# Expert rows: gathered inside the expert loop instead of scattered into per-expert lists ahead of it

## The chip, the cores and the metric

The kernel runs on one core of a Trainium2 chip. A core has engines that work side by side: TensorE for matmuls (PE in the profile, its weight loads PEld), VectorE (DVE), ScalarE (ACT) and GpSimd (POOL), and SyncE (SP), which here only issues DMAs. Each engine takes its instructions in order; engines wait for each other through semaphores. Data moves between HBM and the core's memories by DMA, issued by SP, ACT or POOL. The metric is the device time of one execution in microseconds, the median of several runs.

## The reference, cut to what matters

The input is 8 sequences of 256 tokens, 2048 tokens in all, of 128 features, in float32. One layer is a sandwich: half a feed-forward step, attention, half a feed-forward step with the same weights, and then a second, different layer (the tail). Each feed-forward step is a mixture of eight experts, of which every token uses two:

```python
h = rmsnorm(x @ W_in.T, in_norm_w)
logits = h @ Wr.T
_, idx = jax.lax.top_k(logits + expert_bias, TOP_K)
sel = jnp.take_along_axis(logits, idx, axis=-1)
```

For every token and each of its two experts, the row h is multiplied by the expert's gate and up matrices (128 to 512), goes through silu(gate) times up, and is multiplied by the expert's down matrix (512 to 128) and normed. The two results are weighed by the softmax of sel, normed, multiplied by W_out, and half of that is added to x. So 4096 pairs of token and expert are computed, and which tokens belong to which expert is known only at run time.

## The kernel before

**Order of work.** The program is a straight line: dispatch of the first feed-forward step, its expert loop, its combination, attention (with the second dispatch placed in its later steps), the second expert loop, its combination together with the tail. On PE, DVE, ACT and SP the instructions keep the order in which the program emits them. POOL's order is held for the instructions that ask for it.

**Dispatch** (L311 to L446), once for each group of 128-token tiles. The groups of the first step are `EARLY`, of the second `LATE`. `turned` transposes x, `product` multiplies by W_in and the router at once, `normed` and `scaled` (L373) write the normed row h twice into `hrow`, with the token's number in a 129th column, `choice` finds the two experts, and `places` (L399) counts with small products of 0/1 matrices which place the token has in each expert's list. From it comes `posi` (L428), the row in a DRAM array `hs` with one region of 2304 rows for each expert. `rows` (L430) scatters: for each tile and choice POOL issues one indirect DMA (L433) that writes 128 rows of 516 bytes to the places in `posi`. There are 32 of these in each step.

**Table** (L448 to L519). From the counts of the experts DVE works out which expert and which stretch of its list each of 24 fixed turns treats: 15 pairs of two blocks of 128 rows, and 9 singles. `tab` holds the expert and the first row of every turn, `far` is used to send lanes without a token out of bounds. In the first step, `zeros` (L521) writes zeros behind each expert's list; for the second step, `clear_rows` (L534) clears all of `hs` in 12 large DMAs on ACT's queue during attention.

**Expert loop** (L553 to L660). `fetch_weights` (L561) brings one expert's 832 KB, `fetch_rows` (L570) the turn's rows, both as plain DMAs on SP (L568, L574) with addresses read from `tab`. `turn_rows` transposes the rows (`pht`, L580), `gate` and `up` are `pg` and `pu` (L590), `down` is `py` (L613). Then ACT takes a sum of squares (`ysq`, L623), DVE writes `yrow` (L624), two DVE operations (L628, L631) work out the target row from the fetched token's number, and POOL scatters the result rows into `y2` (L633), one indirect DMA for each block, 39 in a loop. Weights and rows have four buffers, `yrow` two. One turn is:

```python
            sg = gate(t)
            if i + 1 < NT:
                turn_rows(TURNS[i + 1])
            up(t, sg)
            if i < len(pieces):
                pieces[i]()
            if i > 0:
                down(TURNS[i - 1])
            if i + 3 < NT:
                fetch_rows(TURNS[i + 3])
                fetch_weights(TURNS[i + 3])
```

`TURNS` repeats pair, pair, single seven times and ends with a pair and two singles. `pieces` are bits of other work put into the first loop, among them constants for attention that POOL fills with memsets (L800 to L822).

**Attention** is a list of steps, each with a part "a" and a part "b", in which pieces of the second dispatch are placed by hand (L997 to L1109); what remains of it follows after the last step.

Of the kernel before, what the change touches and what calls it, by code (L numbers as in the profile page):

```python
# [10 lines left out]
F32 = mybir.dt.float32  # L11
AF = mybir.ActivationFunctionType
ALU = mybir.AluOpType
# [27 lines left out]
REGION = NTOK + TT  # L41
HS_ROWS = E * REGION + 1
FAR = 1 << 20

EARLY = (0, 2), (2, 2), (4, 4), (8, 4), (12, 4)
# [10 lines left out]
TABLE = 2 * E + E * E + NSING * E + 2 * NT * E + NT + 3 * E  # L56
# [3 lines left out]
def macaron_kernel(ctx: ExitStack, tc: tile.TileContext, a: dict, out: bass.AP):  # L60
# [44 lines left out]
    def pack(name, widths, rows=P):  # L105
# [10 lines left out]
    win, wr_t, inw, eb, tri, slot, base, order, tokid = pack(  # L116
        "pack1", [D, E, 1, E, P, 2, E, E, NCH * TPC * 2]
    )
    tokid = tokid.rearrange("p (t k) -> p t k", k=2).bitcast(I32)
# [4 lines left out]
    zero = const.tile([P, 2 * ROW], F32, tag="zero", name="zero")  # L124
    nc.vector.memset(zero, 0.0)
# [7 lines left out]
    hss = [tc.dram_tile([HS_ROWS, ROW], F32, name=f"hs{f}") for f in range(2)]  # L133
# [170 lines left out]
    thr, upto, nth, tof, eof, tid, vals = cuts((2, E), (E, E), (NSING, E), (NT, E), (NT, E), (NT,), (3, E))  # L304

    hrows = [const.tile([P, TPC, 2, ROW], F32, tag=f"hrow{c}", name=f"hrow{c}") for c in range(NCH)]
    lsel = const.tile([P, NCH * TPC, 2], F32, tag="lsel", name="lsel")
    macc = const.tile([P, len(EARLY) + 1, E], F32, tag="macc", name="macc")
    nc.vector.memset(macc[:, 0, :], 0.0)

    def dispatch(f, i, parts, mp):  # L311
# [4 lines left out]
        x = xs[t0 // TPC][:, t0 % TPC : t0 % TPC + nt, :]  # L316
        hrow = hrows[t0 // TPC][:, t0 % TPC : t0 % TPC + nt]
        slots = slice(t0, t0 + nt)

        def turned():  # L320
            pt = bank(f"pxt_{n}", "sa")
            for t in range(nt):
                nc.tensor.transpose(pt[:, ts(t, P)], x[:, t, :], ident)
            st["xt"] = xntp.tile([P, CT], F32, tag="xnt", name=f"xnt_{n}")
            nc.scalar.copy(st["xt"][:, 0 : nt * P], pt[:, 0 : nt * P])
            st["u"] = mp.tile([P, TPC, D + E], F32, tag="u", name=f"u_{n}")[:, 0:nt]
            st["ss"] = small.tile([P, nt], F32, tag="ss", name=f"ss_{n}")

        def measured():
            bs = small.tile([P, nt, 6], F32, tag="ast", name=f"ast_{n}")  # L330
            mv = small.tile([P, nt, 2], F32, tag="amv", name=f"amv_{n}")
            for t in range(nt):
                nc.vector.bn_stats(bs[:, t, :], x[:, t, :])
# [5 lines left out]
        def product(i):  # L339
            if 2 * i >= nt:  # L340
                return
            pp = bank(f"pin_{n}_{i}", "sa" if f else None)[:, 0 : 2 * (D + E)]
            pp = pp.rearrange("p (j d) -> p j d", j=2)
            for j in range(2):
                nc.tensor.matmul(
                    pp[:, j, :], st["xt"][:, ts(2 * i + j, P)], win_r, start=True, stop=True
                )
            u = st["u"][:, 2 * i : 2 * i + 2]
            nc.scalar.copy(u, pp)
            sq = norm.tile([P, 2, D], F32, tag="sq", name=f"sqin_{n}_{i}")  # L350
            for j in range(2):
                t = 2 * i + j
                nc.scalar.activation(
                    sq[:, j], u[:, j, 0:D], AF.Square, accum_out=st["ss"][:, t : t + 1]
                )

        def normed():
            ri = small.tile([P, nt], F32, tag="ri", name=f"ri_{n}")
            nc.vector.scalar_tensor_tensor(ri, st["ss"], 1.0 / D, st["z"], ALU.mult, ALU.add)
            if f == 0:  # L360
                nc.vector.tensor_copy(hrow[:, :, :, D].bitcast(I32), tokid[:, slots])
# [5 lines left out]
            st["ri"] = ri  # L367

# [4 lines left out]
        def scaled(ts_=range(nt)):  # L373
            for t in ts_:
                u = st["u"][:, t, 0:D].unsqueeze(1).to_broadcast([P, 2, D])
                nc.scalar.activation(hrow[:, t, :, 0:D], u, AF.Copy, scale=st["ri"][:, t : t + 1])
# [22 lines left out]
        def places():  # L399
# [25 lines left out]
            pos = small.tile([P, nt, 2], F32, tag="pos", name=f"pos_{n}")  # L425
            nc.vector.tensor_reduce(pos, both, AX.X, ALU.add)
            st["posi"] = small.tile([P, nt, 2], I32, tag="posi", name=f"posi_{n}")
            nc.vector.tensor_copy(st["posi"], pos)  # L428

        def rows(ts_=range(nt)):  # L430
            for t in ts_:
                for k in range(2):
                    ins = nc.gpsimd.indirect_dma_start(  # L433
                        out=hss[f],
                        out_offset=bass.IndirectOffsetOnAxis(ap=st["posi"][:, t, k : k + 1], axis=0),
                        in_=hrow[:, t, k, :],
                        in_offset=None,
                    )
                    tc.declare_no_dep(ins.ins, group=f"hs{f}", reason="rows of their own")
                    tc.add_to_no_dep_group(f"hs{f}", ins.ins)  # L440
                    tc.keep_in_program_order(ins)

        halves, choices = ([partial(p, i) for i in range(2)] for p in (product, choice))
        if f == 0:
            return turned, *halves, measured, both(normed, logits, scaled), *choices, places, rows
        return turned, *halves, measured, normed, logits, scaled, *choices, places, rows  # L446

    def table(f, parts, mp):  # L448
# [5 lines left out]
        pc = bank(f"pcnt_{f}", "sb")[:, 0:E]  # L454
# [3 lines left out]
        if f == 0:  # L458
            first = t_([P, E], "first", I32)
            nc.vector.tensor_tensor(first, pc, base, ALU.add)  # L460
            zeros(first)
# [1067 lines left out]
```

## Time and profile before

| | us |
|---|---|
| median of 3 runs (lowest, highest) | 659.83 (657.87, 660.45) |
| profiled execution | 673.83 |
| its span | 672.0 |
| dispatch and table of the first step, first loop's start | 0 to 76 |
| first expert loop | 76 to 190 |
| its combination | 190 to 210 |
| attention, most of the second dispatch in it | 210 to 420 |
| end of the second dispatch, table | 420 to 454 |
| second expert loop | 454 to 562 |
| combination and tail | 562 to 672 |

The profile is of one execution, which was some 14 us longer than the median of the others. All times below that name a place ("518.35") are microseconds from the start of its span. A line of the timeline gives start, length, engine, line of the source, operation and operands; in brackets stands how long the engine had been idle, and what ended the wait. `<-remote` and `<-issue` mean that the profile shows no work of this core that the engine waited for. A line of a group gives the number of instructions, their busy time and the mean in nanoseconds, and then the idle time before them. The shown length of a DMA is that of its issue.

### The profile page before, as it was taken

Reading aid. Unit: us, or ns where it says so; the run is one execution under the profiler, and the core shown is the slowest. Engines: PE = TensorE matmul, PEld = TensorE weight load, DVE = VectorE, ACT = ScalarE, POOL = GpSimd, SP = SyncE. Lnnn points to the kernel's source line nnn. Section 1 sums busy time; section 2 is a strip of 40 time slices with the busy share of each in tenths; the row PEclk is TensorE's granted clock in tenths of the full one; section 3 lists DMA queues with packets and bytes.
Section 4 is the critical chain, followed back from the end, with each engine's and each line's share of the span. In section 5 each row is a group of like instructions: output and inputs, shape, how many; then the busy total and the mean of one; then the engine's idle time right before and its main releaser. Section 6 shows DMA issues by size and latency. Waiting matters only on the chain.

```text
span 672.0 us, 11456 instructions
## 1 busy us (share of the span) xinstructions
PE 526.8 (78%) x3945; PEld 415.8 (62%) x3945; DVE 361.6 (54%) x1121; ACT 277.6 (41%) x682; POOL 196.0 (29%) x204
## 2 busy tenths in 40 slices
PE   4521499999957998898898758449999992679996
PEld 3521399999954545555555434329989992458885
DVE  3663156544433555766866545654444451667676
ACT  3451032323323454656664435313222331768355
POOL 0466056633332110101104052522233333511110
PEclk9999999999985799999999779559999997669999
DMA  5012746767721293984930000156767773100002
GB/s 208 32 43 99 248 139 195 240 208 230 230 83 45 41 168 61 148 130 72 143 64 25 9 32 13 36 171 203 239 191 231 237 233 94 50 0 1 1 1 62
DMA packets 57513, 78.26 MB, mean 116 GB/s; under 512 B 5035, under 2 KB 47570, under 8 KB 57328
## 3 DMA queue, kind: packets, MB, share of 16 engines
q1 hardware_dynamic: 33712, 59.02, 30.0%
q10 hardware_dynamic: 19200, 10.04, 9.7%
q0 software_dynamic: 4544, 8.47, 3.6%
q8 instruction: 31, 0.51, 0.3%
q14 instruction: 26, 0.21, 0.1%
HBM read 55.60 MB, written 22.83 MB: 117 GB/s over the span
## 4 chain that ended last, share of the span: by engine, by line
PE 60%; DVE 11%; ACT 9%; DMA 9%; issue 4%; another core or an unknown queue 3%; SPq 1%; POOL 1%; ACTq 0%; DVEq 0%; POOLq 0%
PE pg_f L590 10%; PE py_f L613 10%; PE pu_f L590 9%; PE ps L934 7%; PE po L981 3%; ACT es L971 3%; DMA qk<-heads 3%; PE pvf L1291 2%; PE pgo L1318 2%; DMA y<-yrow_f,idx_f 2%; PE pm L917 2%; DMA w_f<-in_wall_dram 2%; PE pk_m L1235 1%; PE pht_f L580 1%
## 5 line engine op out<-in xcount | busy, mean ns | idle before, releaser
L633 POOL DMA_INDIRECT y<-yrow_f,idx_f x78 | 76.4, 979 | 136.5 <-ACT sg_f L599 79.5
L433 POOL DMA_INDIRECT hs<-hrow,posi_f x64 | 61.9, 966 | 111.3 <-issue 38.2
L934 PE MATMUL ps<-qa,qk 32*128 32x256 f32 x512 | 75.4, 410 | 20.2 <-ACT es L971 17.3
L971 ACT ACTIVATE es<-ps 128x1024 f32<-128x1024 f32 x64 | 65.3, 1020 | 59.4 <-PE ps L934 35.3
L954 DVE TENSOR_REDUCE m<-pm 128x4 f32<-128x1024 f32 x64 | 77.7, 1220 | 20.5 <-PE pm L917 20.5
L917 PE MATMUL pm<-qk 32*128 32x256 f32 x512 | 79.7, 422 | 3.1 <-DMA qk<-heads 1.8
L590 PE MATMUL pg_f<-ht_f,w_f 128*128 128x256 f32 (+1 forms) x384 | 79.7, 352 | 2.9 <-DMA w_f<-in_wall_dram 2.2
L613 PE MATMUL py_f<-w_f,hg_f 128*128 128x128 f32 x624 | 78.2, 276 | 2.4 <-DVE yrow_f L624 2.4
L613 PEld LDWEIGHTS py_f<-w_f,hg_f 128*128 128x128 f32 x624 | 75.2, 192 | 4.6 <-DVE yrow_f L624 3.2
L590 PE MATMUL pu_f<-ht_f,w_f 128*128 128x256 f32 (+1 forms) x384 | 76.9, 344 | 0.0
L606 DVE TENSOR_TENSOR hg_f<-pu_f,sg_f 128x1024 f32<-128x1024 f32 (+1 forms) x48 | 49.2, 1024 | 47.0 <-PE pu_f L590 34.9
L590 PEld LDWEIGHTS pg_f<-ht_f,w_f 128*128 128x128 f32 x384 | 63.1, 197 | 9.6 <-issue 2.9
L934 PEld LDWEIGHTS ps<-qa,qk 32*128 32x128 f32 x512 | 44.5, 189 | 38.4 <-ACT es L971 29.4
L599 ACT ACTIVATE sg_f<-pg_f 128x1024 f32<-128x1024 f32 (+1 forms) x48 | 41.4, 863 | 62.2 <-PE pg_f L590 62.2
L623 ACT ACTIVATE ysq_f<-py_f 128x128 f32<-128x128 f32 x78 | 21.0, 274 | 110.7 <-PE py_f L613 93.4
L590 PEld LDWEIGHTS pu_f<-ht_f,w_f 128*128 128x128 f32 x384 | 61.8, 194 | 6.2
L917 PEld LDWEIGHTS pm<-qk 32*128 32x128 f32 x512 | 47.7, 195 | 7.3 <-issue 3.3
L624 DVE TENSOR_TENSOR yrow_f<-py_f,w_f 128x256 f32<-128x256 f32 (+1 forms) x48 | 18.0, 375 | 54.3 <-ACT ysq_f L623 54.2
L580 PE MATMUL pht_f<-ident,hst_f 128*128 128x128 f32 x78 | 17.5, 290 | 33.0 <-DMA hst_f<-hs 32.9
L582 DVE TENSOR_SCALAR ht_f<-pht_f,pack 128x256 f32<-128x256 f32 (+1 forms) x48 | 20.7, 431 | 33.4 <-PE pht_f L580 33.3
L981 PE MATMUL po<-es,v 128*32 128x256 f32 x512 | 36.6, 401 | 0.0
L966 DVE TENSOR_TENSOR qa<-pmt,qk 128x256 f32<-128x256 f32 x32 | 13.5, 422 | 38.4 <-PE pmt L960 28.9
(257 smaller groups left out, 832.5 us busy)
## 6 DMA issues: line engine op xcount, KB each, us to landing
w_f<-in_wall_dram SPq DMA_DIRECT2D x47, 832.0 KB
hs<-zero ACTq DMA_DIRECT2D x12, 774.0 KB
hst_f<-hs SPq DMA_DIRECT2D x30, 129.0 KB
y_f<-y SPq DMA_DIRECT2D x14, 258.0 KB
pack<-in_pack_dram SPq DMA_DIRECT2D x1, 1729.0 KB
heads<-qkc SPq DMA_DIRECT2D x3, 512.0 KB
qk<-heads SPq DMA_DIRECT2D x12, 128.0 KB
y<-yrow_f,idx_f POOLq DMA_INDIRECT x78
```

Source lines behind the costliest of these rows:

```text
L433: ins = nc.gpsimd.indirect_dma_start(out=hss[f], out_offset=bass.IndirectOffsetOnAxis(ap=st["posi"][:, t, k : k + 1], axis=0), in_=hrow[:, ...
L580: nc.tensor.transpose(pt[:, ts(s, P)], hst[t][:, s, 0:D], ident)
L590: nc.tensor.matmul(ph[:, k, :], w[t][:, o + k * P : o + k * P + P], ht[t], start=True, stop=True)
L599: nc.scalar.activation(sg, pg, AF.Silu)
L606: nc.vector.tensor_mul(hg[t], pu, sg)
L613: nc.tensor.matmul(py[:, s, :], hg[t][:, k, ts(s, P)], w[t][:, 2 * DFF + k * D : 2 * DFF + k * D + D], start=(k == 0), stop=(k == NFC - 1),)
L633: ins = nc.gpsimd.indirect_dma_start(out=y2, out_offset=bass.IndirectOffsetOnAxis(ap=idx[:, s : s + 1], axis=0), in_=yrow[:, s, :], in_off ...
L917: nc.tensor.matmul(sc[:, jj, i, :], qs[c][r, g, col + i * P : col + (i + 1) * P], ks[c][r, g, col : col + S], start=True, stop=True,)
L934: nc.tensor.matmul(sc[:, jj, i, :], ks[c][r, g, col + i * P : col + (i + 1) * P], tops[s][r, :], start=True, stop=True,)
L954: nc.vector.tensor_reduce(m, sc, AX.X, ALU.max, negate=True)
L971: nc.scalar.activation(es, sc, AF.Exp, scale=scale)
L981: nc.tensor.matmul(po[32 * j : 32 * j + 32, :], vs[c][:, (b % 2) * 2 + i, (g % 2) * (H // 2) + (g // 2) * 4 + j, :], ess[s, j // 2][:, j % ...
```

## The change

The lists are not made in DRAM any more. `hs` becomes a plain array of 2048 rows in the order of the tokens, 512 bytes each, written by a linear DMA on SP (`rows`). What is made instead is a list of token numbers in a tile of the core: for every block of the loop, lane by lane, the token that stands there.

The place of a token in its expert's list is cut into a block number (times 128) and a lane (0 to 127). `spread` makes two matrices for each tile and choice, by comparison with a row of counts: `hi` has the token's number plus one where the block number matches, `lo` has a one where the lane matches. The product of both, summed over tiles and choices by PE in PSUM (`mapped`), is a matrix that has in row "block" and column "lane" the token's number plus one, or zero. `maps` keeps one such matrix for each group of tiles. After the table, products of `maps` with 0/1 columns `sel` pick the rows of the blocks that the turns treat (`who`), and two bitwise operations make of it `lists`: the rows to gather from, and the rows to scatter to, out of bounds where there is no token.

In the loop `fetch_rows` is now one indirect DMA on POOL for each block, which gathers 128 rows from `hs` by `lists`; the scatter to `y2` takes its rows from `lists` too. Both keep POOL's program order. The zeros, the clearing and the index operations of the loop are gone. The table is shorter and its expert numbers are ready earlier. The groups of the first dispatch are 4, 4 and 8 tiles in place of 2, 2, 4, 4 and 4. The constants of attention are filled by POOL at the very start, not in the first loop, and the first weights are split into three DMAs in both loops.

```diff
-EARLY = (0, 2), (2, 2), (4, 4), (8, 4), (12, 4)
+EARLY = (0, 4), (4, 4), (8, 8)
...
-    hss = [tc.dram_tile([HS_ROWS, ROW], F32, name=f"hs{f}") for f in range(2)]
+    hss = [tc.dram_tile([NTOK, D], F32, name=f"hs{f}") for f in range(2)]
...
         def scaled(ts_=range(nt)):
             for t in ts_:
-                u = st["u"][:, t, 0:D].unsqueeze(1).to_broadcast([P, 2, D])
-                nc.scalar.activation(hrow[:, t, :, 0:D], u, AF.Copy, scale=st["ri"][:, t : t + 1])
+                nc.scalar.activation(
+                    st["hrow"][:, t], st["u"][:, t, 0:D], AF.Copy, scale=st["ri"][:, t : t + 1]
+                )
+
+        def rows():
+            dst = hss[f][t0 * P : (t0 + nt) * P, :].rearrange("(t p) c -> p t c", p=P)
+            nc.sync.dma_start(dst, st["hrow"])
...
-        def rows(ts_=range(nt)):
-            for t in ts_:
+            part = small.tile([P, 2, nt, 2], I32, tag="part", name=f"part_{n}")
...
+            nc.vector.tensor_copy(st["pos"], part)
+
+        def spread(engine=nc.gpsimd):
+            st["lo"], st["hi"] = (
+                mp.tile([P, nt, 2, P], F32, tag=k, name=f"{k}_{n}", bufs=1) for k in ("lo", "hi")
+            )
+            pos = st["pos"]
+            for t in range(nt):
                 for k in range(2):
-                    ins = nc.gpsimd.indirect_dma_start(
-                        out=hss[f],
-                        out_offset=bass.IndirectOffsetOnAxis(ap=st["posi"][:, t, k : k + 1], axis=0),
-                        in_=hrow[:, t, k, :],
-                        in_offset=None,
+                    tc.keep_in_program_order(
+                        nc.gpsimd.tensor_scalar(
+                            st["hi"][:, t, k],
+                            count128,
+                            pos[:, 0, t, k : k + 1],
+                            tokid[:, t0 + t, k : k + 1],
+                            ALU.is_equal,
+                            ALU.mult,
+                        )
                     )
+                    if engine is nc.gpsimd:
+                        tc.keep_in_program_order(
+                            nc.gpsimd.tensor_scalar(
+                                st["lo"][:, t, k], count, pos[:, 1, t, k : k + 1], None, ALU.is_equal
+                            )
+                        )
+            if engine is nc.vector:
+                row = count.unsqueeze(1).to_broadcast([P, 2, P])
+                for t in range(nt):
+                    nc.vector.tensor_tensor(
+                        st["lo"][:, t], bc_last(pos[:, 1, t], P), row, ALU.is_equal
+                    )
+
+        def mapped():
+            pm = bank(f"pmap_{n}", "sa" if f else None)[:, 0:P]
+            for t in range(nt):
+                for k in range(2):
+                    nc.tensor.matmul(
+                        pm,
+                        st["hi"][:, t, k],
+                        st["lo"][:, t, k],
+                        start=(t == k == 0),
+                        stop=(t == nt - 1 and k == 1),
+                    )
+            nc.scalar.copy(maps[:, i], pm)
...
-        far = t_([P, 2, NT, 2], "far", I32)
-        nc.vector.tensor_scalar(far[:, 0], free, -float(FAR - 1), float(FAR - 1), ALU.mult, ALU.add)
-        nc.vector.tensor_scalar(far[:, 1], free, float(FAR), None, ALU.mult)
-        return tab, far
-
-    def zeros(first):
...
-    def clear_rows(i, n):
...
+        who = bank(f"pwho_{f}", "sb")[:, 0:NBLK]
+        for i in range(len(parts)):
+            nc.tensor.matmul(who, maps[:, i], sel, start=(i == 0), stop=(i == len(parts) - 1))
+
+        num_ = t_([P, NBLK], "number", I32)
+        nc.vector.tensor_scalar(num_, who, -1.0, None, ALU.add)
+        lists = t_([P, 2, NBLK], "lists", I32)
+        sh = [P, 2, NBLK]
+        nc.vector.tensor_tensor(
+            lists, num_.unsqueeze(1).to_broadcast(sh), bc_last(bits[:, 0:2], NBLK), ALU.bitwise_and
+        )
+        return tab, lists
...
         def fetch_rows(t):
             n, m = f"f{f}_{t}", blocks(t)
-            row = nc.values_load(tab[0:1, 0, t : t + 1], engines=[SP], min_val=1, max_val=HS_ROWS - TT)
-            hst[t] = mp.tile([P, 2, ROW], F32, tag="hst", name=f"hst_{n}", bufs=4)[:, 0:m]
-            nc.sync.dma_start(hst[t], hss[f][bass.ds(row, m * P), :].rearrange("(s p) c -> p s c", p=P))
+            hst[t] = mp.tile([P, 2, D], F32, tag="hst", name=f"hst_{n}", bufs=4)[:, 0:m]
+            for s in range(m):
+                b = block(t, s)
+                tc.keep_in_program_order(
+                    nc.gpsimd.indirect_dma_start(
+                        out=hst[t][:, s, :],
+                        out_offset=None,
+                        in_=hss[f],
+                        in_offset=bass.IndirectOffsetOnAxis(ap=lists[:, 0, b : b + 1], axis=0),
+                    )
+                )
...
-            idx = mp.tile([P, 2], I32, tag="idx", name=f"idx_{n}", bufs=3)[:, 0:m]
-            nc.vector.tensor_tensor(
-                idx, hst[t][:, :, D].bitcast(I32), far[:, 0, t, 0:m], ALU.bitwise_and
-            )
-            nc.vector.tensor_tensor(idx, idx, far[:, 1, t, 0:m], ALU.bitwise_or)
...
-                    out_offset=bass.IndirectOffsetOnAxis(ap=idx[:, s : s + 1], axis=0),
+                    out_offset=bass.IndirectOffsetOnAxis(ap=lists[:, 1, b : b + 1], axis=0),
...
+                tc.keep_in_program_order(ins)
...
         for t in TURNS[:3]:
-            for fetch in (fetch_rows, fetch_weights) if f else (fetch_weights, fetch_rows):
-                fetch(t)
+            fetch_rows(t)
+            fetch_weights(t)
...
-                at(25, "a", places)
-                for i in range(TPC):
-                    at(25 + i, "b", partial(rows, [i]))
+                at(20, "b", rows)
+                at(25, "a", places, spread)
+                at(30, "a", mapped)
...
-            stagger([dispatch(0, i, EARLY, gp) for i in range(len(EARLY))], 4)
...
+                for piece in constant_pieces():
+                    piece()
+                with tc.tile_pool(name="front", bufs=2, reuse_waits="tile") as fp:
+                    stagger([dispatch(0, i, EARLY, fp, maps) for i in range(len(EARLY))], 4)
+                    decays[0]()
```

## The prediction

> **What bounds the kernel now.** I read the table of busy time and the chain that ended last first, then a table by stage, then the timeline of the places that the change touches. The page:
>
> ```profile
> span 672.0 us, 11456 instructions
> PE 526.8 (78%) x3945; PEld 415.8 (62%) x3945; DVE 361.6 (54%) x1121; ACT 277.6 (41%) x682; POOL 196.0 (29%) x204
> PE 60%; DVE 11%; ACT 9%; DMA 9%; issue 4%; another core or an unknown queue 3%; SPq 1%; POOL 1%; ACTq 0%; DVEq 0%; POOLq 0%
> L633 POOL DMA_INDIRECT y<-yrow_f,idx_f x78 | 76.4, 979 | 136.5 <-ACT sg_f L599 79.5
> L433 POOL DMA_INDIRECT hs<-hrow,posi_f x64 | 61.9, 966 | 111.3 <-issue 38.2
> ```
>
> PE carries 60% of the chain and POOL 1%, so POOL looks free. An average hides the stages (start:end and length, then PE, PEld, DVE, ACT, POOL busy, PE clock, DMA share, GB/s):
>
> ```profile
> 0.00:76.00 76.00, 23.89 (x97) 20.58 (x97) 36.61 (x205) 24.48 (x74) 31.64 (x41) 1.00 0.32 108
> 76.00:190.00 114.00, 113.14 (x750) 103.60 (x749) 55.19 (x149) 33.96 (x105) 50.66 (x51) 1.00 0.66 206
> 210.00:420.00 210.00, 177.63 (x1860) 108.17 (x1860) 126.81 (x288) 110.64 (x211) 33.69 (x33) 0.92 0.44 73
> 454.00:562.00 108.00, 104.16 (x715) 96.62 (x714) 46.53 (x117) 32.28 (x101) 37.18 (x38) 1.00 0.67 208
> ```
>
> The front (0 to 76) is a chain through DVE and POOL with PE idle; both expert loops (rows two and four) are full of PE work. What a loop can lose is idle PE. The order within one cycle, at turn ends (start, length, engine, line):
>
> ```profile
> 517.25 0.15 DVE L628 TENSOR_TENSOR idx_f<-hst_f,tab_far 128x2 int32<-128x2 int32 x1
> 518.35 0.98 POOL L633 DMA_INDIRECT y<-yrow_f,idx_f  x1 [4.77 <-ACT sg_f L599]
> 519.63 0.98 POOL L633 DMA_INDIRECT y<-yrow_f,idx_f  x1 [0.30 <-issue]
> 521.57 0.38 PE L580 MATMUL pht_f<-ident,hst_f 128*128 128x128 f32 x2
> 522.14 0.98 POOL L633 DMA_INDIRECT y<-yrow_f,idx_f  x1 [1.53 <-issue]
> 523.42 0.98 POOL L633 DMA_INDIRECT y<-yrow_f,idx_f  x1 [0.30 <-issue]
> ```
>
> The down projection of a pair ended at E = 516.05; its two scatters start at 518.35 and 519.63 (0.98 each, 0.30 between: a period of 1.28). The transposes at 521.57, E+5.5, use the rows that were fetched right after that down projection, today by SP, which POOL does not touch. And in the front:
>
> ```profile
> 42.31 0.96 POOL L433 DMA_INDIRECT hs<-hrow,posi_f  x1 [0.30 <-issue]
> 43.41 0.19 DVE L423 TENSOR_TENSOR at_row_f<-prank_f,pack 128x32 f32<-128x32 f32 x1 [4.70 <-remote]
> 62.83 0.38 DVE L499 TENSOR_REDUCE tab_single<-tab_room 128x27 f32<-128x216 f32 x1 [2.45 <-remote]
> ```
>
> DVE stands still 4.70 us until the eighth scatter in a row is done, and the table has eight such gaps while 16 more run: it takes 52.9 to 69.4 here, and 435.8 to 443.6 in the second dispatch, where few scatters run.
>
> **What the skill says.** "Perfetto Trace Analysis", DMA Instruction — SWDGE (GPSIMD): the shown interval of a DMA issued by POOL ends when its descriptors are made, not when data has moved. The trace agrees: 0.98 shown, 2.29 from start to landing for the last scatters of a loop (558.98, 563.07). "DMA: Bandwidth & Descriptors", Anatomy of one DMA — SWDGE (gpsimd) path: about 2.0 us fixed plus bytes/436e3, which for 64 KB of rows is an estimated 2.15; no gather from POOL is in the trace. "TensorE: Matmul & The Clock Gate", What's actually happening: an idle window of about 3.4 us halves PE's rate; here the first eight gate matmuls of a loop take 3.75 us against 1.73 warm.
>
> **The change part by part.** Sums are against the profiled run (673.8, span 672.0), which is 14 us above the median of 659.8; I carry the difference over to the median.
>
> *Both loops, the main step.* Removed: two index operations on DVE per turn (0.15 + 0.16 us, hidden by PE, but 0.26 of the lead to the scatter), the row fetches on SP. Added: 39 gathers per loop on POOL, in program order, the gather of turn i+3 queued behind the scatters of turn i-1, which wait for that turn's yrow. In the repeating cycle pair A, pair B, single C a turn's PE work is 4.57, 5.35 and 3.78 (gate and up 1.73 or 0.89 each, down 1.78 or 0.89, transposes 0.22 or 0.11), together the measured 13.70. After A's down ends at E: scatters at E+2.04 and E+3.32, gathers for the next B at E+4.60 and E+5.88. Needed: E + 3.78 + 1.73 = E+5.51. So even the start of the last gather is 0.37 late, and the stall is 0.37 plus its landing L. B's scatters, then C's one gather: starts at E+9.72, needed at E+10.08 plus the stall: fits. C's scatter and A's two gathers: 0.66 late at L = 2.3, which takes that much from the next stall at B. So one cycle loses 0.37+L in sum, and there are seven (the first three turns are fetched ahead). POOL has 78 × 1.28 = 100 us of work per loop of 107, so it cannot catch up by much.
> L is unknown. Low end: 1.5, if a read of 512-byte rows returns sooner than a scatter's 2.29 completion. High end: 5 to 5.9, which scatters took at three loaded moments (492.84 landed at 498.72). I take 3.0, nearer the unloaded value because weights fill two thirds of DMA time. 7 × 3.37 = 23.6 per loop; at 1.5 it is 13.1, at 5.0 it is 37.6. In loop 0 the placed pieces lengthen the window (its PE runs 114 against 107); I take 4 off. Two loops: **+43**.
>
> *Front.* Removed: 32 scatters, 8 zero fills on two queues, SP's wait for them (its first weight issue 69.83, rows 71.06 behind it, landed 75.4, first gate 76.73). Merging the last eight tiles and no DVE stall should bring the last posi from 52.9 to some 45.6 (4.7 for the stall, the rest ten-odd DVE operations of 0.2). Added behind it: 16 POOL operations of 128x128. None is in the trace: affine select 128x128 took 0.29, so I take 0.35 (5.6 us), bounds 0.15 and 0.6 (-3, +4); POOL ends at 51.5. The lo maps run on DVE meanwhile (8 × 0.42). Products keep up with POOL: +0.5, copy +0.4; the count for the table waits behind them on PE. Table to the expert numbers as in the second dispatch, 5.9: 58.3. Five operations and three products to the lists: 2: 60.3. Gathers from POOL 0.76 later, the second at 62.4, landed 65, gate 66: -10.7. Constants of 14 us moved to POOL's start could hold DVE up to 6 before the first map is wanted. I take **-8** (-13 to +3).
>
> *Attention.* Removed: 12 clears (0.54 of ACT's queue each, 9.7% of DMA): 2 us of PE waiting for head transfers goes. Two stops of all engines beside runs of seven and eight scatters (366.3 to 372.4, 391.3 to 397.0): gone if the scatters cause them, -11; still there in another form, 0; I take -5. Added: three chunks of eight products, 1.78 us each; PE is 85% full, so about half is felt, +3; POOL's maps, two or four DVE operations and a copy lie beside PE. **-4** (-13 to +4).
>
> *Second dispatch.* Added between the last rank (435.4) and the first gate (446.8): two DVE operations, two lo, four hi on POOL (1.4), four products, lists; about 4.5. Removed: the last scatter's landing and the row fetch (442.88 to 445.26), weights behind rows on SP: about 2.5. **+2** (0 to +5).
>
> Sum: 43 - 8 - 4 + 2 = **+33**: 693 for the median, 707 for the profile.
>
> **The rivals.**
> *B, much slower.* Gathers land as late as the loaded scatters, L = 5: 75 - 4 - 8 - 4 + 2 = +61, 721. Every stall is then above 3.4 us and PE falls to half rate after it; if half a window is lost each time, 14 × 1.7 = 24 more, 745. For: the 5.9 us landing fell in a row of four POOL DMAs, and the change makes long rows the rule. Against: slower loops load the queues less.
> *C, faster.* The rows come in time. It decides in one number: twice seven stalls must cost less than about 14 us, so three periods plus L must stay below 4.5 (2.04 + 3p + L - 5.51 < 1). That needs p = 0.98, the 0.30 gap gone, and L near 1.5: 13.6 - 4 of loop loss against -11 front and -12 attention, -13: 646. For: the stops beside scatters are in the chain ("another core or an unknown queue 3%", 21 us). Against: the gap stands between all neighbouring scatters.
> *D, the front gains nothing.* POOL's maps take 0.6 or its constants hold DVE: front +3 in place of -8, 704. For: no row shows these operations. Against: the old front was slowed by POOL anyway.
>
> **How the numbers follow.** A (above, L from 2.3 to 4: 683 to 707) 0.50; B 0.20; C 0.17; D 0.13. 693 is A's. Below 648 lies half of C, above 735 half of B, together under 2 in 10: range 648 to 735. A change below 0.5% (about what a measurement of this kernel can tell from none) can only come from the border of C and A: 0.03. Faster 0.16, slower 0.81.
>
> **What would show it.** In both loops PE idles ahead of the transposes, released by the gather's DMA, some 2 to 3.4 us per cycle, loops of 125 to 131 us in place of 107 to 114; POOL rows of scatter, scatter, gather, gather at 1.28. First gate near 66. No stop of all engines in the attention. I am wrong if PE's transposes wait for nothing, if gathers show a period under 1 us, or if the front grows. The step most likely off is L.

## The result and the profile after

The changed kernel takes 794.35 us (793.66 to 794.85), the kernel before 659.1 (657.87 to 660.45) in the same comparison: a ratio of 1.2051 (95% interval 1.2022 to 1.2079). I had forecast 693 with a range to 735. The direction was right; the size was not, by a factor of four in the loss.

The page of the changed kernel, its span, busy times and the groups that answer to those shown of before:

```profile
span 792.6 us, 11424 instructions
PE 589.8 (74%) x4085; PEld 459.8 (58%) x4085; DVE 348.4 (44%) x968; ACT 275.9 (35%) x687; POOL 289.4 (37%) x326
L678 POOL DMA_INDIRECT y<-yrow_f,tab_lists x78 | 78.3, 1003 | 137.4 <-DVE yrow_f L673 122.7
L617 POOL DMA_INDIRECT hst_f<-hs,tab_lists x78 | 76.4, 980 | 47.7 <-issue 31.1
L456 POOL TENSOR_SCALAR hi_f<-pack,pos_f,pack 128x128 f32<-128x128 f32 x64 | 52.3, 821 | 99.9 <-DVE pos_f L446 34.5
L467 POOL TENSOR_SCALAR lo_f<-pack,pos_f 128x128 f32<-128x128 f32 x44 | 26.3, 597 | 0.0
L629 PE MATMUL pht_f<-ident,hst_f 128*128 128x128 f32 x78 | 23.5, 327 | 77.2 <-DMA hst_f<-hs,tab_lists 77.1
```

The last line is the loops' loss as a wait: 77.1 us in which PE stands before a transpose whose rows have not arrived. The fourth and fifth are what I had no row for: a map operation on POOL takes 0.82 us (hi) or 0.60 us (lo), not 0.35.

Where the time went is read from the turning points of the span, against the profile shown and against a second profile of the kernel before (e0, below). Lengths in us:

| stretch | before, as shown | before again | after | after less before again |
|---|---|---|---|---|
| start to first gate matmul | 76.7 | 67.8 | 91.2 | +23.4 |
| first loop, to its last down matmul | 115.0 | 114.9 | 158.8 | +43.9 |
| to the end of attention's last `po` | 226.3 | 215.3 | 230.2 | +14.9 |
| end of the second dispatch, to the first gate matmul | 28.8 | 28.7 | 46.3 | +17.6 |
| second loop | 113.4 | 114.3 | 155.9 | +41.6 |
| combination and tail | 111.8 | 110.6 | 110.1 | -0.5 |
| span | 672.0 | 651.6 | 792.6 | +141.0 |

So the loops lost 85.5 us, and the two dispatches, which I had down for a gain of 10 together, lost 56.

The two loops of the changed kernel by window (start:end and length; PE, PEld, DVE, ACT, POOL busy; PE clock, DMA share, GB/s), and below them both loops of the kernel before in its second profile:

```profile
91.00:250.00 159.00, 129.55 (x757) 113.30 (x757) 50.04 (x106) 35.48 (x106) 71.30 (x73) 0.89 0.45 135
527.00:682.00 155.00, 123.93 (x730) 109.87 (x730) 43.23 (x70) 33.10 (x100) 68.67 (x70) 0.89 0.46 137
```

```profile
68.00:183.00 115.00, 113.89 (x757) 104.28 (x757) 55.68 (x151) 34.12 (x105) 52.12 (x53) 1.00 0.66 206
427.00:541.00 114.00, 110.20 (x733) 101.35 (x732) 47.79 (x116) 32.93 (x100) 36.19 (x37) 0.98 0.69 214
```

In the first loop PE makes the same matmuls in both (757), but is busy 15.7 us longer at a clock of 0.89, and idle 28 us more. One cycle in the timeline of the changed kernel, after the down projection that ended at 537.84:

```profile
539.40 1.02 POOL L678 DMA_INDIRECT y<-yrow_f,tab_lists  x1 [13.78 <-DVE yrow_f L673]
540.72 1.00 POOL L678 DMA_INDIRECT y<-yrow_f,tab_lists  x1 [0.31 <-issue]
541.63 1.89 PE L639 MATMUL pg_f<-ht_f,w_f 128*128 128x256 f32 x8
542.03 0.99 POOL L617 DMA_INDIRECT hst_f<-hs,tab_lists  x1 [0.30 <-PE py_f L662]
543.33 0.97 POOL L617 DMA_INDIRECT hst_f<-hs,tab_lists  x1 [0.30 <-issue]
545.49 0.30 PE L629 MATMUL pht_f<-ident,hst_f 128*128 128x128 f32 x1 [1.97 <-DMA hst_f<-hs,tab_lists]
548.69 0.48 PE L629 MATMUL pht_f<-ident,hst_f 128*128 128x128 f32 x1 [2.90 <-DMA hst_f<-hs,tab_lists]
548.96 3.62 PE L639 MATMUL pu_f<-ht_f,w_f 128*128 128x256 f32 x8
```

Scatter, scatter, gather, gather, 1.3 us apart; the first gather's rows are there 3.5 us after its start, the second's some 5.3 us. PE waits 1.97 and then 2.90 us, and the eight up matmuls behind these waits take 3.62 us, where the eight gate matmuls before them, of the same shape, took 1.89. The granted clock is 1.00 up to 548.0 and 0.50 from there to 554.7.

### The profile page after: what moved, and what is told of

Read it like the earlier page. It is cut to its first block, busy times and chain, and to the rows that moved or that the text cites. A ratio compares the mean times of both kernels' runs of the same rounds, so it can differ in the third digit from the quotient of the medians.

```text
span 792.6 us, 11424 instructions
## 1 busy us (share of the span) xinstructions
PE 589.8 (74%) x4085; PEld 459.8 (58%) x4085; DVE 348.4 (44%) x968; ACT 275.9 (35%) x687; POOL 289.4 (37%) x326
## 5 line engine op out<-in xcount | busy, mean ns | idle before, releaser
L678 POOL DMA_INDIRECT y<-yrow_f,tab_lists x78 | 78.3, 1003 | 137.4 <-DVE yrow_f L673 122.7
L639 PE MATMUL pu_f<-ht_f,w_f 128*128 128x256 f32 (+1 forms) x384 | 95.1, 400 | 0.0
L617 POOL DMA_INDIRECT hst_f<-hs,tab_lists x78 | 76.4, 980 | 47.7 <-issue 31.1
L456 POOL TENSOR_SCALAR hi_f<-pack,pos_f,pack 128x128 f32<-128x128 f32 x64 | 52.3, 821 | 99.9 <-DVE pos_f L446 34.5
L662 PE MATMUL py_f<-w_f,hg_f 128*128 128x128 f32 x624 | 82.6, 286 | 1.6 <-DVE yrow_f L673 1.6
L662 PEld LDWEIGHTS py_f<-w_f,hg_f 128*128 128x128 f32 x624 | 80.7, 203 | 4.4 <-DVE yrow_f L673 1.9
L629 PE MATMUL pht_f<-ident,hst_f 128*128 128x128 f32 x78 | 23.5, 327 | 77.2 <-DMA hst_f<-hs,tab_lists 77.1
L639 PEld LDWEIGHTS pu_f<-ht_f,w_f 128*128 128x128 f32 x384 | 75.1, 230 | 10.0
L629 PEld LDWEIGHTS pht_f<-ident,hst_f 128*128 128x128 f32 x78 | 11.6, 152 | 88.3 <-DMA hst_f<-hs,tab_lists 58.2
L482 PE MATMUL pmap_f<-lo_f,hi_f 128*128 128x128 f32 x128 | 37.9, 432 | 17.7 <-POOL lo_f L467 11.8
```

What stands on the lines that cost most here:

```text
L456: nc.gpsimd.tensor_scalar(st["hi"][:, t, k], count128, pos[:, 0, t, k : k + 1], tokid[:, t0 + t, k : k + 1], ALU.is_equal, ALU.mult,)
L482: nc.tensor.matmul(pm, st["hi"][:, t, k], st["lo"][:, t, k], start=(t == k == 0), stop=(t == nt - 1 and k == 1),)
L617: nc.gpsimd.indirect_dma_start(out=hst[t][:, s, :], out_offset=None, in_=hss[f], in_offset=bass.IndirectOffsetOnAxis(ap=lists[:, 0, b : b ...
L639: nc.tensor.matmul(ph[:, k, :], w[t][:, o + k * P : o + k * P + P], ht[t], start=True, stop=True)
L662: nc.tensor.matmul(py[:, s, :], hg[t][:, k, ts(s, P)], w[t][:, 2 * DFF + k * D : 2 * DFF + k * D + D], start=(k == 0), stop=(k == NFC - 1),)
L678: ins = nc.gpsimd.indirect_dma_start(out=y2, out_offset=bass.IndirectOffsetOnAxis(ap=lists[:, 1, b : b + 1], axis=0), in_=yrow[:, s, :], i ...
```

## The experiments

Two theories stood against each other for the loops: **Q**, the gathers are late because of their place in POOL's queue, behind scatters that wait for the down projection; and **W**, they land slowly beside the weights, wherever they stand. For the dispatches **P**, POOL's slow map operations hold up what is queued behind them and the PE products that use them. The ratios below are to the kernel before in the same comparison; its own time was 652 to 653 us in those of e0 to e8 and 671 in that of e9, so ratios, not times, are compared across.

**e0, the kernel before once more.**

> The kernel before, unchanged, for a second profile. If the stops of DVE and of all engines beside runs of scatters belong to executions under the profiler, the profile again takes 670 to 676 us against 659 without it, with the same stops at the same scatters. If they were a chance of that one execution, the profile takes 657 to 663 without them. If they are real in every execution, the profile would agree with the median, and it did not before.

A span of 651.6, and neither kind of stop is there. In the profile that I had argued from, DVE's wait for the third rank had been 4.70 us and ended by nothing of this core; in the second profile of the same kernel it is 2.42 and ended by PE:

```profile
40.47 0.19 DVE L423 TENSOR_TENSOR at_row_f<-prank_f,pack 128x32 f32<-128x32 f32 x1 [2.42 <-PE prank_f L413]
67.79 1.62 PE L590 MATMUL pg_f<-ht_f,w_f 128*128 128x256 f32 x3 [0.62 <-issue]
```

The table's eight gaps are gone too, and the first gate is at 67.8, not 76.7. The profiled execution took 653.4 us, and the median of the others in this comparison is 651.7. The profile of e7 (below), which has the same scatters, shows no stop of this kind either. As far as these profiles tell, the stops were of one execution, not of the kernel. What caused them stays open.

**e1, gathers first.**

```diff
+            if i + 3 < NT:
+                fetch_rows(TURNS[i + 3])
             if i > 0:
                 down(TURNS[i - 1])
             if i + 3 < NT:
-                fetch_rows(TURNS[i + 3])
                 fetch_weights(TURNS[i + 3])
```

> One edit: in a turn of the loop the gathers of turn i+3 are issued before the down projection and scatters of turn i-1, so that on POOL they stand one turn earlier. Theory Q (a gather is late because it stands in POOL's queue behind scatters that wait for the down projection, which adds some 5 us of stall per cycle of three turns and lets PE's clock fall): PE's waits for gathered rows fall from 77 us to below 20, both loops from 152-156 to 110-118 us, PE clock in them back to 1.00, total about 80 us shorter, near 715. Rival W (gathers are late because they land slowly beside the weights, whatever their place in the queue): landing stays at 3.5 us or grows, a wait of over 1 us per cycle remains, and the total falls by less than 40.

714.7 us, ratio 1.0938 (1.0875 to 1.1002). PE's waits for rows in all, their number and the longest:

```profile
PE pht_f L629 <- DMA hst_f<-hs,tab_lists: 25.7, 12, 8.1
```

They were 77.1. Of the 25.7, 19.0 lie ahead of the loops; the total is over the 20 that I expected. The loops take 120.4 and 114.9 at a clock of 0.98, the first a little longer than expected. The same 78 gathers on the same engine land no sooner (4.5 at the median in place of 3.6, from the 28 whose landing the profile has), but once they stand one turn earlier they cost 5.5 us in the first loop and 0.6 in the second, where they had cost 43.9 and 41.6. That speaks for Q.

**e2, the weights of four turns only.**

```diff
             n = f"f{f}_{t}"
+            if TURNS.index(t) >= 4:
+                w[t] = w[TURNS[TURNS.index(t) - 4]]
+                return
```

> The changed kernel without the weight fetches after the fourth turn of each loop (later turns multiply by the weights that lie in the buffers, so part of the computation is replaced); the order on POOL stays. Theory Q: landing of a gather falls from 3.5 towards 2.5 us, but the last gather of a cycle still starts after its rows are needed, so 2.5 to 3.5 us of stall per cycle remain, loops of 125 to 135 us in place of 152-156, total 40 to 55 us shorter. Rival W: the waits for rows go altogether, loops near 110, total about 85 us shorter.

From the fifth turn on this version multiplies by weights that were fetched for earlier turns; only its times are of use. 748.0 us, ratio 1.1465 (1.1383 to 1.1547). From the page of this run, the transposes and the time from issue to landing in us, and its two loops by window:

```profile
L632 PE MATMUL pht_f<-ident,hst_f 128*128 128x128 f32 x78 | 22.1, 308 | 47.8 <-DMA hst_f<-hs,tab_lists 47.4
hst_f<-hs,tab_lists POOLq DMA_INDIRECT x78, 2.5
y<-yrow_f,tab_lists POOLq DMA_INDIRECT x78, 2.3
93.00:225.00 132.00, 117.66 (x752) 103.84 (x753) 49.33 (x106) 35.46 (x106) 70.85 (x72) 0.97 0.12 33
505.00:636.00 131.00, 114.88 (x733) 102.26 (x733) 43.27 (x71) 33.09 (x100) 69.31 (x70) 0.97 0.12 34
```

A gather lands in 2.5 us at the median when these weights are not fetched, and the loops still take 132.5 and 130.8: 17.6 and 16.5 over the kernel before. The prediction's sum, seven cycles of 0.37 + L less 4 in the first loop, gives 16.1 and 20.1 at L = 2.5, which is near; but its parts differ. Of the 47.4 us of waits 19.3 lie ahead of the loops, which leaves 28.1, or 2.0 per cycle, where the sum has 2.87 and I had expected 2.5 to 3.5. PE is besides busy 3.8 and 4.7 us longer than before, at a clock of 0.97; with the waits this makes 36.6, against a loss of 34.1. So the queue order alone makes a loss of about 17 us per loop, and the weight traffic adds some 26 to it by late landing and by what follows from that. W is wrong as the only cause and right as an amplifier.

**e8, rows gathered five turns ahead,** the order within a turn kept:

```diff
-            hst[t] = mp.tile([P, 2, D], F32, tag="hst", name=f"hst_{n}", bufs=4)[:, 0:m]
+            hst[t] = mp.tile([P, 2, D], F32, tag="hst", name=f"hst_{n}", bufs=6)[:, 0:m]
...
-        for t in TURNS[:3]:
+        for i, t in enumerate(TURNS[:5]):
             fetch_rows(t)
-            fetch_weights(t)
+            if i < 3:
+                fetch_weights(t)
...
+            if i + 5 < NT:
+                fetch_rows(TURNS[i + 5])
             if i + 3 < NT:
-                fetch_rows(TURNS[i + 3])
                 fetch_weights(TURNS[i + 3])
```

> The changed kernel with rows gathered five turns ahead in place of three (six buffers), the order scatters, then gathers in a turn kept. Theory Q says that lateness is all: two more turns of distance are some 9 us, more than the stalls, so the waits go and the loops come to 113 to 122 us, total near 720, as with the gathers first. If what helped there was only that the gathers no longer share a moment with the scatters, the landings stay bunched and the loops stay over 135.

705.5 us, ratio 1.0793 (1.0734 to 1.0852); loops of 113.8 and 110.3. The wait of PE in all, number and longest, in the view of the waits:

```profile
PE pht_f L629 <- DMA hst_f<-hs,tab_lists: 18.8, 4, 8.8
```

```profile
93.00:207.00 114.00, 113.05 (x757) 103.78 (x757) 49.75 (x106) 34.18 (x105) 71.18 (x73) 1.00 0.62 190
485.00:595.00 110.00, 109.22 (x733) 101.40 (x733) 43.22 (x70) 33.09 (x100) 68.06 (x69) 0.98 0.64 194
```

The four waits left are those ahead of the loops. POOL's queue is as before, scatter ahead of gather, and its landings are no sooner (4.9 at the median, from 21 of the 78); only the distance changed. PE is full and its clock is back. With e1 this shows that lateness was all of the loops' loss.

**e3, the power operation ahead of the maps,** in the attention's list of steps:

```diff
-                at(25, "a", places, spread)
-                at(30, "a", mapped)
+                at(25, "a", places)
+                at(25, "b", spread)
+                at(28, "a", mapped)
...
-                at(32, "a", mapped)
+                at(31, "a", mapped)
```

> Two edits of place in the attention's steps: POOL's maps of a group of tiles are issued after POOL's small power operation of the next group's norm, not before it, and the products of the maps move with them. Theory P (ACT and DVE wait for the power operation, which stands behind 16 map operations of 0.6 to 0.8 us on POOL, and everything waits for them): the two stops of all engines of about 10 us each in the last third of the attention go, total 15 to 21 us shorter. Rival (POOL's map operations slow DVE and PE down beside them[...]): the stops move with the maps, total within 4 us.

776.5 us, ratio 1.1904 (1.184 to 1.1969): 17.8 us below the changed kernel in plain times, about 10 by the ratios. By the profiles, the stretch to attention's end takes 217.7 in place of 230.2. The stop that it removes, in the changed kernel:

```profile
425.53 0.59 POOL L467 TENSOR_SCALAR lo_f<-pack,pos_f 128x128 f32<-128x128 f32 x1
426.10 1.03 POOL L153 TENSOR_TENSOR ri_f<-ri_f,mhalf 128x4 f32<-128x4 f32 x1
427.16 0.69 ACT L379 ACTIVATE hrow_f<-u_f,ri_f 128x128 f32<-128x128 f32 x2 [10.48 <-POOL ri_f L153]
428.81 0.80 PE L980 MATMUL ps<-qa,qk 32*128 32x256 f32 x2 [10.44 <-ACT es L1017]
```

Sixteen map operations run on POOL from 415.2 to 426.1; the power of the next group's norm, a 1 us operation, stands behind them, ACT stands before the row scaling that needs it, and attention's exponentials stand behind that on ACT. A second stop of this kind is at 464.8. In e3 both are gone. The gain in the stretch, 12.5, is under the 15 to 21 that I expected. The plain times overstate it: the profile's first loop is 149.7 us in e3 and 150.3 in e5 (below), 9 less than in the changed kernel, though neither edit touches that loop. What makes this difference stays open.

**e4, all maps on DVE.**

```diff
-                    tc.keep_in_program_order(
-                        nc.gpsimd.tensor_scalar(
-                            st["hi"][:, t, k],
...
+                    nc.vector.tensor_scalar(
+                        st["hi"][:, t, k],
...
+                    nc.vector.tensor_scalar(
+                        st["lo"][:, t, k], count, pos[:, 1, t, k : k + 1], None, ALU.is_equal
+                    )
```

together with the places of `mapped` as in e3, which free the buffers in time.

> All map operations (hi and lo) are made by DVE, one 128x128 operation each, in place of POOL; the products of the maps stand a few steps earlier in the attention so that the buffers come free. Theory P (POOL's maps, 0.6 to 0.8 us each and 108 of them, hold up PE in the first dispatch and POOL's power operation in the attention): the first gate comes near 75 in place of 91, the attention loses its two 10 us stops, the end of the second dispatch is 4 us shorter; total 32 to 42 us shorter than the changed kernel. Rival D (DVE is what the dispatch is short of): some 13 us of DVE work are added to each dispatch, and the total falls by less than 15.

771.3 us, ratio 1.1809 (1.1733 to 1.1885). The group lines for the maps in this run:

```profile
L455 DVE TENSOR_SCALAR hi_f<-pack,pos_f,pack 128x128 f32<-128x128 f32 x64 | 22.2, 347 | 4.5 <-PE pmap_f L471 4.3
L463 DVE TENSOR_SCALAR lo_f<-pack,pos_f 128x128 f32<-128x128 f32 x64 | 18.3, 286 | 0.0
```

The first gate comes at 78.1 in place of 91.2, near what I expected, and the stretch to attention's end takes 223.6 in place of 230.2. The end of the second dispatch, however, is as long as it was (46.1), and the total fell by 27.4 (from 798.7, the changed kernel in the same comparison), less than the 32 to 42 forecast. An operation on DVE is 0.35 and 0.29 us, not the 0.2 that I had counted with, 40 us in both dispatches. In the attention part of it seems to be felt: the stretch is 6 us longer than in e3, where POOL makes the maps. "GPSIMD Engine Reference" of the Trainium skill, Key points, says that DVE is about twice as fast at elementwise work; here it is 2.4 times for hi (0.82 to 0.35) and 2.1 for lo (0.60 to 0.29).

**e5, the products of the maps later on PE.** Maps on POOL as in the change, in the first dispatch only:

```diff
-            late = [spread, mapped] if i < len(parts) - 1 else [partial(spread, nc.vector), mapped]
+            late = [spread if i < len(parts) - 1 else partial(spread, nc.vector)]
+            late += 3 * [lambda: None] + [mapped]
```

> In the first dispatch the products of a group's maps are issued three steps later, behind the next groups' input products and ranks on PE; POOL still makes the maps. If PE's queue is what carries POOL's slowness into the next group (input products of the last group stand behind map products that wait for POOL), the first gate comes at 79 to 83 in place of 91, total 8 to 12 us shorter. If POOL's own 36 us of map operations set the pace, under 4 us.

The first gate comes at 81.6, within the 79 to 83 expected; the total of two runs is 780.6, ratio 1.1957 (1.1829 to 1.2085), which does not tell it from the change by itself. What it removes, two lines of the changed kernel, and below them the same products in e5:

```profile
32.95 0.79 PE L482 MATMUL pmap_f<-lo_f,hi_f 128*128 128x128 f32 x2 [0.57 <-POOL lo_f L467]
33.54 3.20 PE L352 MATMUL pin_f<-win_r,xnt_f 128*128 128x136 f32 x16
```

```profile
25.73 3.54 PE L352 MATMUL pin_f<-win_r,xnt_f 128*128 128x136 f32 x16 [3.24 <-ACT xnt_f L329]
```

In the changed kernel the input products of the last eight tiles start at 33.54, behind map products that wait for POOL pair by pair from 22 to 33; in e5 at 25.73. So 9.6 us of the 23.4 that the front lost were the order on PE.

**e6 and e9, the mends together.** e6 has the gathers first (e1), the maps on DVE (e4), their products later (e5, and behind the last group's choice in the second dispatch), and asks for the second and third turn's weights only after the lists. e9 has the gathers five turns ahead (e8) in place of first within the turn.

```diff
+        tab2 = t_([P, NT], "tab2", I32)
+        nc.vector.tensor_copy(tab2, et)
+        return (tab, tab2), lists
...
-            e = nc.values_load(tab[0:1, t : t + 1], engines=[SP], min_val=0, max_val=E - 1)
+            e = nc.values_load(tab[t != TURNS[0]][0:1, t : t + 1], engines=[SP], min_val=0, max_val=E - 1)
```

> The changed kernel with the gathers first (as in the first run), the maps on DVE, their products later on PE in the first dispatch and behind the last group's choice in the second, and the second and third turn's weights asked for only after the lists are made, so that the first gathers do not stand behind 2.5 MB of weights. If the causes found so far add up: 73 for the gathers, 35 for the maps, 4 to 8 for the first gathers, so about 115 us below the changed kernel, within 2 to 4% above the kernel before. If something else in the change costs time that these do not touch, it stays over 5% slower; if the removed scatters and clears were worth what I had put on them, it is faster than the kernel before.

> The version with all mends (maps on DVE, their products later, weights of the second and third turn after the lists), with rows gathered five turns ahead in place of gathers first within the turn. If the mends add up, the loops take 110 to 114 us each and the total is 6 to 10 us below the version with the gathers first, 1.035 to 1.045 times the kernel before; what then remains lies ahead of the two loops alone, some 15 us each. If the DVE maps and the distant gathers disturb each other, no shorter than that version.

e6 takes 687.1 us, ratio 1.0514 (1.0444 to 1.0583); e9 702.1 us, ratio 1.0499 (1.0436 to 1.0561). Both miss what I expected to the slow side; e6, at over 5%, falls into the case in which something else in the change costs time that these edits do not touch. In e6 the loops take 117.6 and 114.8, and most of what remains over the kernel before lies outside them: the first gate at 82.6 (+14.8), 41.4 us from attention's end to the second loop (+12.6), and 5 in the attention. The two edits of the front do not add up: e4 alone has its first gate at 78.1. The first gathers of e6 start at 73.14, where e0 asks for its rows at 64.16; and they take 6.7 us to the transpose (79.82), where e0's rows take 2.3 (66.48). So asking for two turns' weights later was no cure. In e9 the five turns brought nothing more; its loops take 123.9 and 123.4, with PE waiting 10.1 us for `yrow`, in a comparison in which the kernel before was slower too. Whether that comes from the chip's state, or from maps and gathers together, was not tried. Even mended, the change does not reach the kernel before.

**e7, the kernel before without the clears.**

```diff
-    hss = [tc.dram_tile([HS_ROWS, ROW], F32, name=f"hs{f}") for f in range(2)]
+    hss = 2 * [tc.dram_tile([HS_ROWS, ROW], F32, name="hs")]
...
-                for i, s in enumerate(clears):
-                    at(s, "b", partial(clear_rows, i, len(clears)))
```

> The kernel before, with one array for the rows of both steps, so that the 12 clearing DMAs of 10 MB in the attention fall away and nothing else (what lies behind a list is then an older row or a zero of the first step, finite in both cases, and is sent out of bounds as before). My prediction priced the removed clears at 2 us, from PE's waits for the head transfers beside them. If that is right: 1 to 4 us faster than the kernel before. If the clears are hidden altogether: within 1 us. If ACT's queue and the DMA share they take matter more: over 5 us faster.

651.1 us against 653.4, ratio 0.9955 (0.9933 to 0.9977): 1.5 to 4.4 us faster, and the lowest ratio here. The prediction priced the clears at 2 us, from PE's waits for the head transfers; in the profiles these waits fall from 2.2 us (e0) to 1.1, so that the size is confirmed and the reason in part. It leans on the lists of the second step not reaching far beyond what the first step wrote, which these inputs grant and others need not.

The changed kernel once more, in the comparison of e4 to e6:

> The changed kernel unchanged, as the reference of this chip: 1.20 times the kernel before, gathers landing in 3.5 us at the median, first gate near 91.

798.7 us, ratio 1.2234 (1.2132 to 1.2335), first gate at 92.2, loops of 159.6 and 159.2, landing 3.6 at the median. So the ratio of one version differs by 1.5% between two comparisons, and smaller steps above rest on the stretches of their profiles.

## Why the prediction was right or wrong

**Both loops, +43 predicted, +85.5 measured; mechanism right, three terms mis-sized.** The order of scatters and gathers, the period (1.28 predicted, 1.3 measured) and the place of the stall were as worked out, and e1, e2 and e8 show the cause. The first term is L, which I took as 3.0. It is 2.5 in e2, but beside the weights the gather that sets the stall is the last of four DMAs in a row, and in the cycle shown it lands after 5.3. The second is the 0.37 by which the last gather was to start too late. In the cycle shown it starts at 543.33, and PE would have been ready for its rows at 543.52: 0.2 to spare. The transpose of the other block takes 0.3 more off the wait, so that an estimate from this cycle is L - 0.5 per cycle: 2.0 at L = 2.5, which is what e2 has, and 4.8 at 5.3, where the cycle shown has 4.87. That the sum with 0.37 came near in e2 was luck: too long a wait stood in for a clock that I had left out. In the changed kernel PE's waits within the loops are 77.1 less the 18.5 ahead of them, 58.6 us, or 4.2 per cycle in place of 3.37. The third term is the clock. I had put it at nothing in the likeliest case and counted it in rival B alone, where every stall was to be above 3.4 us. But the stall comes as two waits with 0.3 us of work between, neither as long as that, and the clock falls behind them; PE's busy time rises by 15.7 and 13.7 us, 29.4 together, at a clock of 0.89. "TensorE: Matmul & The Clock Gate", What's actually happening, speaks of an idle window, not of one gap; in this trace 0.3 us of work inside the wait did not keep the clock up. 58.6 + 29.4 = 88, against 85.5. For the loops rival B was nearer (71 after its own 4, 95 with the clock): its 24 for the clock was close to the 29.4, its waits of 75, before the 4, were longer than the 58.6.

**Front, -8 predicted, +23.4 measured; wrong.** Four of its terms failed. First, the gain: DVE's stop of 4.7 and the slow table were read from an execution that the second profile does not repeat (e0). From one stop and eight gaps of one execution I had made a property of scatters in a row. In the second profile the table is done at 58.1, while POOL still scatters to 62.8, and the front ends at 67.8. Second, the map operations: 0.35 from an affine select, against 0.82 and 0.60; the last 16 took 13.8 us (56.2 to 70.0), not 5.6. Third, "products keep up with POOL": I priced only the last group's maps. The 32 maps of the two groups before it, 11 us each, pass their slowness to PE, which keeps its order, and so to the next group's input products and ranks (e5). What I should have named is what stands behind the products that wait. Fourth, the first gathers: I had 2.6 us from the start of the second to its landing, and from its start at 83.42 to its transpose at 90.11 it took 6.7.

**Attention, -4 predicted, +14.9 measured to its end; wrong.** That POOL's maps would "lie beside PE" left out the other work on POOL's queue: the power operation that ACT and DVE wait for (e3). The two stops beside scatters that I took half of as a gain were not in the second profile. The clears' 2 us were right (e7). With no maps ahead of the power operation the stretch is 217.7, against 215.3 with the clears: the products' +3 is of the right size, though no run has it by itself.

**Second dispatch, +2 predicted, +17.6 measured; wrong.** "About 4.5" for what is added was the step that failed; it had the operations, and not what waits in the queues behind them. Products at a low clock (0.53 from 480 to 527; eight products take 3.75 us, where I had 1.78) stand ahead of a copy on ACT behind which the last group's norm waits (DVE idle 3.42 at 495.4), the maps of the last two groups take POOL 5.5 and 3.6, and the first gathers start at 517.0, after weights asked for at 513.7, and the transpose waits to 524.65. These are readings of one trace. e6 reorders them and brings 5 of the 17.6; what holds the rest was not taken apart further.

**The rivals.** C, faster, is excluded: the period did not fall, and L did not reach 1.5. D was right in its cause (maps at 0.6 or above, the front losing) and too small in size, +3 for a front of +23.4. B's 721 to 745 left the dispatches at -10; with the +56 that they cost it would have reached 787 to 811. The loops' error alone would have led to 735, the edge of the range. It was left behind because the dispatches had been given bounds between -13 and +5, as if their parts could not stand in each other's queue.

## What to carry to other kernels

When work moves to an engine that keeps its order, ask two things of every instruction put there: what was already on that queue and who waits for it, and which engine keeps its own order behind the result. A gather on POOL cost next to nothing here, with POOL busy for 62% of the loop, once it was issued early enough: one turn earlier in the queue, or two turns more of distance, was worth some 73 and 82 us by the ratios, though no gather landed sooner for it. Before an idle time of a single profile is booked as a gain, compare that execution with the median; if it is 2% longer, take another profile.

## What the runs showed of the hardware that I had not expected

An operation of one float32 tensor of 128x128 and two per-partition scalars takes POOL 0.82 us, with one scalar 0.60; DVE takes 0.35 and 0.29. A gather of 128 rows of 512 bytes lands 2.5 us after its start at the median where the weight fetches are left out (e2), and 3.6 (up to 7.6) beside them. Two waits of 1.97 and 2.90 us with a third of a microsecond of work between them were enough for PE's next eight matmuls to run at half rate.
